# Reciprocal roots in the second layer of a graph network kernel: from an integer trick on VectorE to powers on GpSimd, with the planner's bookings re-set

## The chip, the cores and the metric

The kernel runs on one core of one Trainium2 chip. The metric is the device time in microseconds (us) of one execution. The core's engines run their own queues of instructions, each strictly in order: PE (TensorE, matmuls; PEld is its weight load), DVE (VectorE), ACT (ScalarE), POOL (GpSimd, which here also issues the indirect gathers) and SP (which issues plain DMAs). An instruction that waits for another engine holds up everything behind it in its own queue.

## The reference: what is computed

Two layers over a graph of 3125 nodes with 256 features and 50,000 edges (sorted by target). Layer 0 adds a graph convolution, a linear attention with an MLP, and a soft mixture of 8 experts. Layer 1, cut to what the change touches:

```python
xn = _layernorm(x)
x = x + gnn(xn, src, dst) + hyper(xn)        # edge attention with an MLP; hyperbolic branch
x = x + moe(_layernorm(x))                   # a shared MLP, and 2 of 8 private experts

# gnn: y = (softmax over a node's edges of clip(q.k), times v) @ Wp; x1 = feat + y
h = _layernorm(x1, ln_g, ln_b)               # reciprocal root of the variance: "g"
out = x1 + gelu(h @ W1.T + b1) @ W2.T + b2

# hyper: proj and logmap0 divide by the norm of a row, again and again
proj(x)    = where(n > maxnorm, x / n * maxnorm, x)
expmap0(u) = tanh(n) * u / n                 # n = norm of the row
logmap0(p) = arctanh(clip(n)) * p / n
```

In the kernel the hyperbolic branch needs three reciprocal norms per node, called nn, n3 and n4 after their tiles, each from a sum of squares that stands in a tile of 125 rows and 1 to 4 columns.

## The kernel before

The nodes are cut into 25 tiles of 125 rows, grouped into 7 chunks of four tiles (the last has one). x and its normed copy stay in SBUF.

*The planner.* The order of instructions isn't written out by hand. Each piece of work is a generator that yields `Op(engine, cost, after, take, give)` (line 68) ahead of the instructions that it issues. `Flow.run` (line 87 on) keeps, engine by engine, the time at which the engine would be free by these booked costs in us, adds 0.2 for each hand-over and 1.28 where ACT must load another function table, and always issues the op that could start first; ties go to the lower urgency. `take` and `give` name buffers with their counts. The booked costs thus decide only the order in which each engine's queue is filled; the chip then runs the queues in order at its own speed.

*Layer 0* (until some 1200 us). Per tile, 17 indirect gathers on POOL (L1063) fetch neighbour rows, and PE adds them up (L1092), in groups of six, six and five. Between them PE runs the layer's MLP (L683 and L697, stream `mlp_stream`, line 636) and then the soft experts (L1171 "fp0" and "fp1", L1183 "fy").

*Layer 1, edges* (some 1205 to 2025 us). For each of 75 groups of five or six blocks of edges: POOL gathers k and v into one of three kvg buffers (L1504), PE expands q (L1540), DVE multiplies it with k (L1544), sums (L1563) and clips (L1568), ACT takes the exponential (L1570), DVE scales v (L1573), and PE sums into the target nodes (L1581). After the third group of a tile the sums are divided, turned and multiplied by Wp. Three streams run beside it:

- `mlp_stream` with name "g": mean and variance per tile (L644, L645), the chunk's reciprocal root (L650, L651), the normed rows (L654), turning, the up-projection hp_g (L683) with a gelu on ACT (L675), the down-projection dn_g (L697). The same function serves layer 0 under the name "m".
- `hyper`, tile by tile, with the root nn for each pair of tiles (L1671 to L1674), a division of 512 columns on DVE (L1684), and transposes and matmuls on PE (cat, oT, ft).
- `hyper_end`, chunk by chunk, with the roots n3 (L1718 to L1720) and n4 (L1733 to L1739).

*Layer 1, experts*. When all chunks are normed again (`route_in`), the router sorts rows to experts, POOL scatters them, and PE runs 32 blocks of two private experts' matmuls (L2059, L2074). The shared MLP (`shared`, L1985 and L1999) fills PE meanwhile.

*The root*, `rsqrt` (line 287), is a bit trick and three Newton rounds, all on DVE: a shift and a multiply-add on integers (L291, L292) and three times L295, L296, L297. It is called with 1 to 4 columns; the caller books 2.1 or 2.3 us for it with its neighbours.

Of the kernel before, what the change touches and what calls it, by code (L numbers as in the profile page):

```python
# [7 lines left out]
F32 = mybir.dt.float32  # L8
# [3 lines left out]
OP = mybir.AluOpType  # L12
# [8 lines left out]
P = 125  # L21
# [129 lines left out]
def kernel(ctx: ExitStack, tc: tile.TileContext, a: dict, out: bass.AP):  # L151
# [71 lines left out]
    def row(pool, name, parts=P):  # L223
# [41 lines left out]
    part = keep.tile([128, 1], F32, name="part")  # L265
    nc.gpsimd.iota(part, pattern=[[0, 1]], base=0, channel_multiplier=1,
                   allow_small_or_imprecise_dtypes=True)
    tiny = keep.tile([128, 1], F32, name="tiny")
    nc.vector.memset(tiny, 1e-15)
    rank8 = keep.tile([P, NE], F32, name="rank8")  # L270
# [15 lines left out]

    def rsqrt(v, n, name, parts=P):

        y = small.tile([parts, n], F32, tag=f"rsy{n}", name=f"rsy_{name}", bufs=6)
        g = small.tile([parts, n], F32, tag=f"rsg{n}", name=f"rsg_{name}", bufs=6)  # L290
        nc.vector.tensor_scalar(g.bitcast(I32), v.bitcast(I32), 1, None, op0=OP.arith_shift_right)  # L291
        nc.vector.tensor_scalar(y.bitcast(I32), g.bitcast(I32), -1, 0x5F3759DF,  # L292
                                op0=OP.mult, op1=OP.add)
        for _ in range(3):
            nc.vector.scalar_tensor_tensor(g, y, -0.5, v, op0=OP.mult, op1=OP.mult)  # L295
            nc.vector.tensor_tensor(g, g, y, OP.mult)  # L296
            nc.vector.scalar_tensor_tensor(y, g, 1.5, y, op0=OP.add, op1=OP.mult)  # L297
        return y

    def turned(dst_, src_, nt, name, nk=2, g=None, b=None):  # L300

# [334 lines left out]
    def mlp_stream(c, inputs, name, pool_of, w1, w2, g, b, b1, done, start=None):  # L636

        t0, nt = CHUNKS[c]
        n = nt * P
        mv = small.tile([P, 4, 2], F32, tag=f"mv_{name}", name=f"mv_{name}{c}", bufs=2)  # L640
        for j in range(nt):
            m = yield Op("DVE", 0.6, [inputs[t0 + j]])
            st = small.tile([P, 6], F32, tag="st", name=f"st_{name}{c}_{j}")
            nc.vector.bn_stats(st, XN[c][:, j, :])  # L644
            nc.vector.bn_aggr(mv[:, j, :], st)  # L645
            m2 = yield Op("DVE", 0.42, [m])
            nc.vector.tensor_tensor(X[c][:, j, :], X[c][:, j, :], XN[c][:, j, :], OP.add)
        m = yield Op("DVE", 2.1, [m])
        var = small.tile([P, 4], F32, tag="rs", name=f"var_{name}{c}")
        nc.vector.tensor_scalar(var[:, :nt], mv[:, :nt, 1], 1e-5, None, op0=OP.add)  # L650
        rs = rsqrt(var[:, :nt], nt, f"{name}{c}")  # L651
        for j in range(nt):
            m = yield Op("DVE", 0.36, [m, m2])
            nc.vector.tensor_scalar(XN[c][:, j, :], XN[c][:, j, :], mv[:, j, 0:1],  # L654
                                    rs[:, j : j + 1], op0=OP.subtract, op1=OP.mult)
        both = []
        mk = yield Op("PE", 0.48 * nt, [m] + ([start] if start else []), take=["mm", "mm", "mlp"])
        pt = [mm_tile([128, 512], f"tr_{name}_{c}_{k}") for k in range(2)]
        for k in range(2):
            for j in range(nt):  # L660
                nc.tensor.transpose(pt[k][:, j * P : (j + 1) * P],
                                    XN[c][:, j, k * 128 : (k + 1) * 128], ident[:P, :P])
        for k in range(2):
            m = yield Op("ACT", 0.56, [mk], take=["hT"] if k == 0 else [], give=["mm"])
            if k == 0:
                hT = pool_of().tile([128, 2, 4 * P], F32, tag="hT", name=f"hT_{name}_{c}")
            nc.scalar.activation(hT[:, k, :n], pt[k][:, :n], AF.Identity,
                                 bias=col(b, k), scale=col(g, k))
        hid, todo, acts = [], [], []
        def gelu():  # L670
            mk, ps, q = todo.pop(0)
            act = yield Op("ACT", 0.75, [mk], give=["mm"], table="gelu")
            acts.append(act)
            hm = pool_of().tile([128, 4 * P], F32, tag="hid", name=f"hid_{name}{c}_{q}", bufs=8)
            nc.scalar.activation(hm[:, :n], ps[:, :n], AF.Gelu, bias=col(b1, q))  # L675
            hid.append(hm)

        for h in range(8):
            mk = yield Op("PE", 0.0035 * n, [m], take=["mm", "hid"],
                          give=["hT", "mlp"] if h == 7 else [])  # L680
            ps = mm_tile([128, 512], f"hp_{name}{c}_{h}")
            for k in range(2):
                nc.tensor.matmul(ps[:, :n], w1[:, k, h * 128 : (h + 1) * 128], hT[:, k, :n],  # L683
                                 start=(k == 0), stop=(k == 1))
# [758 lines left out]
    def layer1(lists):  # L1443
# [23 lines left out]
        for m in range(6):  # L1467
# [9 lines left out]

        flow = Flow(kvg=3, S=3, Sb=2, ST=2, q3=2, qe=2, ed=1, mm=2, nm=3, z=1, cat=2, r=2,
                    oT=1, ft=5, ch=2, sc=1, mlp=1, hT=1, hid=8,
                    mh=8, rhid=8, rw=2, xr=2, xrT=2, yr=2, to=3)  # L1480
        attended_ = [Mark() for _ in range(T)]
        mlp_, hyp_ = [Mark() for _ in CHUNKS], [Mark() for _ in CHUNKS]

# [128 lines left out]
        def hyper(t, pair, ch):  # L1612
# [6 lines left out]
            if t == t0:  # L1619
# [1 line left out]
                z = pair["z"] = lp.tile([128, 6, 2 * P], F32, tag="z", name=f"z_{t}")  # L1621
                nc.sync.dma_start(out=z[:, :, : nt * P], in_=ztab[:, :, t0 * P : (t0 + nt) * P])
                for i in range(6):
                    mk = yield Op("ACT", 0.43, [m])
                    nc.scalar.activation(z[:, i, : nt * P], z[:, i, : nt * P], AF.Relu,
                                         bias=bh[:, i : i + 1], scale=bs[:, i : i + 1])
                pair["ready"].set(mk)
# [4 lines left out]
            for i in range(4):  # L1632
                s, h = divmod(i, 2)
                last = i == 3 and t == t0 + nt - 1
                mk = yield Op("PE", 0.75 if s == 0 else 1.4, [pair["ready"]],
                              take=["nm"] + (["cat"] if i == 0 else []),
                              give=["z"] if last else [])
                po = nm_tile([P, 3, 128], f"cat_{t}_{i}")
# [27 lines left out]
                                    AX.X, OP.add)  # L1666
            s12 = ch["s12"][:, j : j + 1]
            if t == t0 + nt - 1:
                m = yield Op("DVE", 2.3, [m, full])
                nn = lp.tile([P, 2], F32, tag="nn", name=f"nn_{t}", bufs=2)[:, :nt]  # L1670
                nc.vector.tensor_reduce(nn, pair["n2"][:, :nt, :], AX.X, OP.add)  # L1671
                nc.vector.tensor_scalar(nn, nn, MIN_NORM ** 2, None, op0=OP.max)
                y = rsqrt(nn, nt, f"nn{t}")
                nc.vector.tensor_scalar(ch["s12"][:, j + 1 - nt : j + 1], y, ATANH_MAXN, 1.0,  # L1674
                                        op0=OP.mult, op1=OP.min)
                pair["scale"].set(m)
# [5 lines left out]
            for q in range(2):  # L1682
# [10 lines left out]
            sq = lp.tile([P, 512], BF16, tag="sq", name=f"sq3_{t}")  # L1693
            nc.scalar.activation(sq, r.rearrange("p q d -> p (q d)"), AF.Square,
                                 accum_out=ch["n3"][:, j : j + 1])
            m = yield Op("PE", 0.96, [m], take=["mm"], give=["r"])
            pt = mm_tile([128, 4, P], f"oT_{t}")
            for k in range(4):
                nc.tensor.transpose(pt[:, k, :], r[:, k, :], ident[:P, :P])
# [13 lines left out]

        def hyper_end(c, ch):
            t0, nt = CHUNKS[c]
            m = yield Op("DVE", 2.3, ch["done"])
            n3, s3, n4 = ch["n3"][:, :nt], ch["s3"][:, :nt], ch["n4"][:, :nt]
            nc.vector.tensor_scalar(n3, n3, MIN_NORM ** 2, None, op0=OP.max)  # L1718
            y = rsqrt(n3, nt, f"n3{c}")
            nc.vector.tensor_scalar(s3, y, ATANH_MAXN, 1.0, op0=OP.mult, op1=OP.min)  # L1720
            ends = []
            for j in range(nt):
# [4 lines left out]
            for j in range(nt):  # L1727
# [1 line left out]
                sq = lp.tile([P, 512], BF16, tag="sq", name=f"sq4_{t0 + j}")  # L1729
                nc.scalar.activation(sq[:, :C], ch["ft"][j], AF.Square,  # L1730
                                     accum_out=ch["n4"][:, j : j + 1])
            m = yield Op("DVE", 2.3, [m])
            nc.vector.tensor_scalar(n4, n4, MIN_NORM ** 2, None, op0=OP.max)  # L1733
            y = rsqrt(n4, nt, f"n4{c}")
            nc.vector.tensor_tensor(n4, n4, y, OP.mult)
            m = yield Op("ACT", 0.22, [m])
            nc.scalar.activation(n4, n4, AF.Tanh)
# [230 lines left out]
        def shared(c):  # L1968
# [10 lines left out]

            for h in range(8):  # L1980
                tag = ("mm", "qe")[h % 2]
                mk = yield Op("PE", 0.0035 * n, [turned_[c], moe_], take=[tag, "mh"])
                ps = ps_tile(tag, [128, 512], f"hp_s{c}_{h}")
                for k in range(2):
                    nc.tensor.matmul(ps[:, :n], R["w1"][:, k, h * 128 : (h + 1) * 128],  # L1985
# [4 lines left out]
            for j in range(nt):  # L1990
                for q in range(0, 8, 4):
                    if j == 0 and q == 4:
                        yield from gelu()
                    m = yield Op("PE", 1.75, [acts[q + 3]], take=["nm"] if q == 0 else [],
                                 give=["mh"] * 8 if j == nt - 1 and q == 4 else [])
                    if q == 0:
                        po = nm_tile([P, C], f"dn_s{c}_{j}")
                    for i in range(q, q + 4):
# [320 lines left out]
```

## Time and profile before

| | |
|---|---|
| median of 11 runs | 2757.36 us (2752.74 to 2761.26) |
| the profiled execution | 2755.13 us, its span 2753.3 us |
| busy over the span | PE 2496.5 us (91%), DVE 1389.6 (50%), POOL 1157.6 (42%), ACT 968.3 (35%) |
| mean granted PE clock | 0.966 |
| layer 0, gathers of POOL | 250.5 to 828 us |
| layer 1, first to last gather | 1229.2 to 1997.3 us |
| POOL gathers of layer 1, L1504 | 425, 461.1 us busy, 309.2 us of idle time before them |

How to read it: busy time is time in which an instruction ran. A row of a group gives the line, the engine, the operation, written and read tile, count, then busy us and mean ns, then the engine's idle time ahead of such instructions with what ended most of it. A row of waits gives who waited, `<-` for whom, us in total, how many times, and the longest. A wait for several events is put down to the last of them. PE's ends are modelled, so a busy PE isn't PE at its peak.

### The profile page before, as it was taken

To read this page: it belongs to the slowest core of one execution; us is meant where nothing else is said; L and a number is where in the kernel's file an instruction comes from. 1 tells how busy PE (TensorE), PEld (TensorE's weight loads), DVE (VectorE), ACT (ScalarE), POOL (GpSimd) and SP (SyncE) were. 2 spreads that over 40 slices of the span, in tenths; PEclk is the share of its full clock that TensorE was granted. 3 is DMA by queue.
4 is the path that set the end of the run, shared out by engine and by line. 5 is a ranking of instruction groups with operands and counts; after the bars stand their busy time and mean duration, and the time that the engine had idled before them with its cause. 6 is when DMAs were issued, how large, how long until landed. Compare 5 with 4: busy or idle time off the path is not lost. (4 is left out here: it accounts for less than half of the span.)

```text
span 2753.3 us, 32241 instructions
## 1 busy us (share of the span) xinstructions
PE 2496.5 (91%) x11409; PEld 1816.6 (66%) x11409; DVE 1389.6 (50%) x3497; ACT 968.3 (35%) x2001; POOL 1157.6 (42%) x1145
## 2 busy tenths in 40 slices
PE   4889989999999999987778888889898999999998
PEld 3556776666666555565556666667576678888885
DVE  6365123453633334267898888888886101111103
ACT  4773112232223333344335444444532222222221
POOL 3002777777770000025665655565601822222220
PEclk9989989999999999998899999999999999999999
DMA  4425565576661015137676655565610355555545
GB/s 111 154 91 175 169 211 165 166 218 177 206 183 35 1 56 149 37 97 249 203 225 193 209 186 181 185 213 176 211 46 1 85 186 188 197 198 188 195 144 144
DMA packets 186968, 427.01 MB, mean 155 GB/s; under 512 B 31403, under 2 KB 116523, under 8 KB 178604
## 3 DMA queue, kind: packets, MB, share of 16 engines
q0 software_dynamic: 80688, 281.78, 33.1%
q1 hardware_dynamic: 103448, 140.79, 16.2%
q10 hardware_dynamic: 2660, 2.29, 0.3%
q8 instruction: 92, 1.51, 0.2%
q14 instruction: 80, 0.66, 0.1%
HBM read 358.95 MB, written 65.74 MB: 154 GB/s over the span
## 5 line engine op out<-in xcount | busy, mean ns | idle before, releaser
L1504 POOL DMA_INDIRECT kvg<-kvtab,el x425 | 461.1, 1085 | 309.2 <-issue 103.7
L1063 POOL DMA_INDIRECT msg<-hs,el x425 | 421.7, 992 | 322.0 <-DMA hot<-S 190.6
L1175 ACT ACTIVATE fh<-fp,bnh,bns 128x500 f32<-128x500 f32 (+1 forms) x224 | 160.7, 723 | 372.6 <-PE fp L1171 370.8
L1581 PE MATMUL es<-kvg,S 128*125 128x264 f32 x850 | 220.2, 411 | 51.1 <-DVE kvg L1573 50.6
L2047 ACT ACTIVATE rhid<-rh,rw 128x256 f32<-128x256 f32 x256 | 121.5, 474 | 338.2 <-PE rh L2059 338.2
L2059 PE MATMUL rh<-xrT,rw 128*128 128x256 f32 x1024 | 237.4, 380 | 0.0
L2074 PE MATMUL ry<-rw,rhid 128*128 128x256 f32 x1024 | 231.5, 379 | 0.0
L1186 DVE SCALAR_TENSOR_TENSOR x<-fy,f_w,x 125x256 f32<-125x256 f32 x200 | 96.2, 482 | 262.2 <-PE fy L1183 261.7
L1581 PEld LDWEIGHTS es<-kvg,S 128*125 128x125 f32 x850 | 163.3, 198 | 98.1 <-DVE kvg L1573 67.0
L1092 PEld LDWEIGHTS <-S 128*125 128x125 bf16 x1275 | 153.3, 138 | 94.5 <-issue 82.5
L1540 PE MATMUL qe<-q,ST 125*128 125x256 bf16 x1275 | 173.1, 277 | 44.8 <-DVE kvg L1544 39.0
L2074 PEld LDWEIGHTS ry<-rw,rhid 128*128 128x128 f32 x1024 | 194.6, 190 | 26.9 <-issue 0.5
L2059 PEld LDWEIGHTS rh<-xrT,rw 128*128 128x128 f32 x1024 | 189.7, 190 | 28.6 <-ACT rhid L2047 5.0
L2081 DVE TENSOR_TENSOR yr<-ry,rw 128x256 f32<-128x256 f32 x64 | 27.2, 424 | 357.7 <-PE ry L2074 357.7
L1183 PE MATMUL fy<-f_Wo,fh 128*125 128x256 f32 x800 | 205.3, 380 | 1.2 <-DVE x L1186 0.8
L1092 PE MATMUL es<-msg,S 128*125 128x256 bf16 x1275 | 183.1, 276 | 24.7 <-DMA msg<-hs,el 23.9
L1171 PE MATMUL fp<-fh,f_W 128*128 128x500 f32 (+1 forms) x448 | 187.0, 545 | 0.3 <-ACT fh L1175 0.3
L1171 PE MATMUL fp<-xT_f,f_W 128*128 128x500 f32 (+1 forms) x448 | 186.0, 541 | 0.0
L1540 PEld LDWEIGHTS <-ST 125*128 125x128 bf16 x1275 | 125.5, 99 | 81.4 <-issue 48.6
L1183 PEld LDWEIGHTS fy<-f_Wo,fh 128*125 128x125 f32 x800 | 142.2, 188 | 55.9 <-issue 34.4
L1299 POOL TENSOR_TENSOR xn<-xn,row_bp 125x1024 f32<-125x1024 f32 (+1 forms) x7 | 13.8, 1977 | 379.8 <-DVE hx L1273 192.5
L1544 DVE TENSOR_TENSOR kvg<-qe,kvg 128x512 f32<-128x512 f32 (+1 forms) x225 | 142.8, 651 | 26.5 <-PE qe L1540 21.1
(422 smaller groups left out, 4225.4 us busy)
## 6 DMA issues: line engine op xcount, KB each, us to landing
db<-dlT SPq DMA_DIRECT2D x25, 544.0 KB
ST<-dlT SPq DMA_DIRECT2D x25, 544.0 KB
hot<-S SPq DMA_DIRECT2D x50, 187.5 KB
Sb<-hot SPq DMA_DIRECT2D x50, 187.5 KB
ztab<-z SPq DMA_DIRECT2D x18, 500.0 KB
z<-ztab SPq DMA_DIRECT2D x12, 750.0 KB
xs<-pad SPq DMA_DIRECT2D x1, 8224.0 KB
xr<-xs SPq DMA_DIRECT2D x32, 257.0 KB
```

Source lines behind the costliest of these rows:

```text
L1063: nc.gpsimd.indirect_dma_start(out=msg[:, i, :], out_offset=None, in_=hs3_rows, in_offset=bass.IndirectOffsetOnAxis(ap=el[:, b, g0 + i : g ...
L1092: nc.tensor.matmul(blk["po"], S[:, i, :], msg[:, i, r * C : (r + 1) * C], start=(g0 + i == 0 and r == 0), stop=(g0 + i == LE - 1 and r == 2))
L1171: nc.tensor.matmul(ps[q][:, :n], self.ws[e][i][:, k, q * 128 : (q + 1) * 128], h[:, k, :n], start=(k == 0), stop=(k == 1))
L1175: nc.scalar.activation(nxt[:, q, :n], ps[q][:, :n], AF.Relu, bias=self.sh[i][:, 2 * e + q : 2 * e + q + 1], scale=self.sc[i][:, 2 * e + q ...
L1183: nc.tensor.matmul(po, nxt[:, k, j * P : (j + 1) * P], self.ws[e][2][:, k, :], start=(k == 0), stop=(k == 1))
L1504: nc.gpsimd.indirect_dma_start(out=kvg[:, i, : 2 * C], out_offset=None, in_=kvtab, in_offset=bass.IndirectOffsetOnAxis(ap=el[:, b, g0 + i ...
L1540: nc.tensor.matmul(pq[i0][:, i, :], ST[:P, g0 + i0 + i, :], blk["q3"][:, r, :], start=(r == 0), stop=(r == 2))
L1544: nc.vector.tensor_tensor(kvg[:, i0 : i0 + k, :C], pq[i0][:, :k, :], kvg[:, i0 : i0 + k, :C], OP.mult)
L1581: nc.tensor.matmul(blk["pa"], S[:, i, :], kvg[:, i, C:], start=(g0 + i == 0), stop=(g0 + i == LE - 1))
L2047: nc.scalar.activation(hid[-1][:, q % 2, :], ps, AF.Gelu, bias=w1[:, 8 * C + q : 8 * C + q + 1])
L2059: nc.tensor.matmul(ps, w1[:, k * 4 * C + h * 128 : k * 4 * C + (h + 1) * 128], xrT[:, k, :], start=(k == 0), stop=(k == 1))
L2074: nc.tensor.matmul(po, hid[k // 2][:, k % 2, r * 128 : (r + 1) * 128], w2[:, k * C : (k + 1) * C], start=(k == 0), stop=(k == 7))
```

## The change

It has two halves. In layer 1 the four kinds of root (nn, n3, n4, and the variance of the MLP "g") are taken by a new generator, `rsqrt_by_power`: POOL raises the operand to the power -0.5, elementwise, and DVE refines it by one Newton round of three instructions. As DVE and POOL now hand over, the one booked op of 2.1 or 2.3 us becomes up to four: the instructions ahead on DVE, the power on POOL (booked 0.65), the round on DVE (0.5), the instructions behind. Layer 0's MLP keeps `rsqrt`. Second, several bookings get other values: the up-projection of `mlp_stream` (both layers), the relu of the hyperbolic input, its transposes and matmuls; and the shared MLP takes a token "shared", so that only one chunk of it can be under way. Some small tiles get more buffers. The core of the diff:

```diff
+    minus_half = keep.tile([128, 4], F32, name="minus_half")
+    nc.vector.memset(minus_half, -0.5)
...
+    def rsqrt_by_power(v, n, name, m):
+
+        y = small.tile([P, n], F32, tag=f"rpy{n}", name=f"rpy_{name}", bufs=8)
+        g = small.tile([P, n], F32, tag=f"rpg{n}", name=f"rpg_{name}", bufs=8)
+        m = yield Op("POOL", 0.65, [m])
+        nc.gpsimd.tensor_tensor(y, v, minus_half[:P, :n], OP.pow)
+        m = yield Op("DVE", 0.5, [m])
+        nc.vector.scalar_tensor_tensor(g, y, -0.5, v, op0=OP.mult, op1=OP.mult)
+        nc.vector.tensor_tensor(g, g, y, OP.mult)
+        nc.vector.scalar_tensor_tensor(y, g, 1.5, y, op0=OP.add, op1=OP.mult)
+        return y, m
...
-        mv = small.tile([P, 4, 2], F32, tag=f"mv_{name}", name=f"mv_{name}{c}", bufs=2)
+        mv = small.tile([P, 4, 2], F32, tag="mmv", name=f"mv_{name}{c}", bufs=len(CHUNKS))
...
+        if name == "m":
+            m = yield Op("DVE", 2.1, [m])
...
+        else:
+            m = yield Op("DVE", 0.17, [m])
+            var = small.tile([P, 4], F32, tag="mvar", name=f"var_{name}{c}", bufs=len(CHUNKS))
+            nc.vector.tensor_scalar(var[:, :nt], mv[:, :nt, 1], 1e-5, None, op0=OP.add)
+            rs, m = yield from rsqrt_by_power(var[:, :nt], nt, f"{name}{c}", m)
...
-            mk = yield Op("PE", 0.0035 * n, [m], take=["mm", "hid"],
+            mk = yield Op("PE", 0.0039 * n, [m], take=["mm", "hid"],
...
-                    mh=8, rhid=8, rw=2, xr=2, xrT=2, yr=2, to=3)
+                    mh=8, shared=1, rhid=8, rw=2, xr=2, xrT=2, yr=2, to=3)
...
-                    mk = yield Op("ACT", 0.43, [m])
+                    mk = yield Op("ACT", 0.55, [m])
...
-                mk = yield Op("PE", 0.75 if s == 0 else 1.4, [pair["ready"]],
+                mk = yield Op("PE", 0.48 if s == 0 else 0.86, [pair["ready"]],
...
-                m = yield Op("DVE", 2.3, [m, full])
+                m = yield Op("DVE", 0.4, [m, full])
...
-                y = rsqrt(nn, nt, f"nn{t}")
+                y, m = yield from rsqrt_by_power(nn, nt, f"nn{t}", m)
+                m = yield Op("DVE", 0.17, [m])
...
-            m = yield Op("PE", 0.96, [m], take=["mm"], give=["r"])
+            m = yield Op("PE", 0.62, [m], take=["mm"], give=["r"])
...
-            m = yield Op("DVE", 2.3, ch["done"])
+            m = yield Op("DVE", 0.17, ch["done"])
...
-            y = rsqrt(n3, nt, f"n3{c}")
+            y, m = yield from rsqrt_by_power(n3, nt, f"n3{c}", m)
+            m = yield Op("DVE", 0.17, [m])
...
-            m = yield Op("DVE", 2.3, [m])
+            m = yield Op("DVE", 0.17, [m])
...
-            y = rsqrt(n4, nt, f"n4{c}")
+            y, m = yield from rsqrt_by_power(n4, nt, f"n4{c}", m)
+            m = yield Op("DVE", 0.17, [m])
...
-                mk = yield Op("PE", 0.0035 * n, [turned_[c], moe_], take=[tag, "mh"])
+                mk = yield Op("PE", 0.0035 * n, [turned_[c], moe_],
+                              take=[tag, "mh"] + (["shared"] if h == 0 else []))
...
-                                 give=["mh"] * 8 if j == nt - 1 and q == 4 else [])
+                                 give=["mh"] * 8 + ["shared"] if j == nt - 1 and q == 4 else [])
```

More of the change, by code (lines that the diff above doesn't have):

```diff
@@ L287, in rsqrt @@
     def rsqrt(v, n, name, parts=P):
-        y = small.tile([parts, n], F32, tag=f"rsy{n}", name=f"rsy_{name}", bufs=6)
-        g = small.tile([parts, n], F32, tag=f"rsg{n}", name=f"rsg_{name}", bufs=6)
+        y = small.tile([parts, n], F32, tag=f"rsy{n}", name=f"rsy_{name}", bufs=6 if n < 9 else 1)
+        g = small.tile([parts, n], F32, tag=f"rsg{n}", name=f"rsg_{name}", bufs=6 if n < 9 else 1)
         nc.vector.tensor_scalar(g.bitcast(I32), v.bitcast(I32), 1, None, op0=OP.arith_shift_right)
@@ L647, in mlp_stream @@
             nc.vector.tensor_tensor(X[c][:, j, :], X[c][:, j, :], XN[c][:, j, :], OP.add)
[L648 to L651, printed above, removed]
+        if name == "m":
+            m = yield Op("DVE", 2.1, [m])
+            var = small.tile([P, 4], F32, tag="rs", name=f"var_{name}{c}")
+            nc.vector.tensor_scalar(var[:, :nt], mv[:, :nt, 1], 1e-5, None, op0=OP.add)
+            rs = rsqrt(var[:, :nt], nt, f"{name}{c}")
+        else:
+            m = yield Op("DVE", 0.17, [m])
+            var = small.tile([P, 4], F32, tag="mvar", name=f"var_{name}{c}", bufs=len(CHUNKS))
+            nc.vector.tensor_scalar(var[:, :nt], mv[:, :nt, 1], 1e-5, None, op0=OP.add)
+            rs, m = yield from rsqrt_by_power(var[:, :nt], nt, f"{name}{c}", m)
         for j in range(nt):
```

## The prediction

> **What bounds the kernel now.** I read the table of windows first, because shares of the whole span mix two layers and the experts. Columns: window, its length, then busy us (and instructions) of PE, PEld, DVE, ACT and POOL, then PE's granted clock, DMA share, GB/s.
>
> ```profile
> 1300.00:1400.00 100.00, 72.02 (x391) 55.75 (x389) 80.92 (x157) 36.84 (x103) 63.83 (x58) 0.88 0.69 213
> 1400.00:1500.00 100.00, 82.69 (x441) 61.46 (x442) 92.76 (x166) 48.76 (x112) 62.53 (x58) 0.93 0.65 204
> ...
> 2200.00:2400.00 200.00, 194.79 (x900) 166.16 (x899) 21.51 (x53) 48.05 (x100) 55.65 (x60) 0.98 0.54 190
> 2400.00:2600.00 200.00, 200.00 (x954) 174.61 (x953) 22.61 (x56) 53.15 (x112) 55.35 (x56) 1.00 0.55 194
> ```
>
> Behind 2130 us PE is the bound (busy 605.6 of 624 us), and between 400 and 1200 us too (96% to 100%). From 1300 to 2000 us, the second layer's edges, it isn't: seven such windows sum to DVE 614.5 busy of 700, PE 585.2, so PE idles 114.8 us. PE's work behind that stage is fixed, so what shortens the stage should reach the end. Whom PE waits for is in its list of waits, 1300 to 2000 us (total, times, longest):
>
> ```profile
> PE es L1581 <- DVE kvg L1573: 40.6, 43, 3.4
> PE qe L1540 <- DVE kvg L1544: 36.3, 38, 5.3
> PE hp_g L683 <- ACT hT_g L667: 14.3, 3, 5.0
> ```
>
> The first two rows, with three small ones, make 81 of the 115 us. So DVE is the engine to relieve. Its own 85 us of idle are waits for ACT above all:
>
> ```profile
> DVE r L1684 <- ACT r L1681: 22.8, 10, 3.9
> DVE sums L1592 <- ACT sums L1589: 10.3, 11, 2.1
> ```
>
> **The roots on DVE.** The old root is 11 dependent small instructions. Three of their groups in the same stretch (busy, mean ns, then idle before them):
>
> ```profile
> L295 DVE SCALAR_TENSOR_TENSOR rsg_nn<-rsy_nn,nn 125x2 f32<-125x2 f32 x33 | 5.4, 162 | 1.1
> ...
> L295 DVE SCALAR_TENSOR_TENSOR rsg_g<-rsy_g,var_g 125x4 f32<-125x4 f32 x15 | 2.5, 163 | 0.5
> ...
> L291 DVE TENSOR_SCALAR rsg_nn<-nn 125x2 int32<-125x2 int32 x11 | 1.9, 169 | 0.4
> ```
>
> One takes 162 ns and 33 ns pass before it (1.1 us over 33): a step of 0.195 us, as the timeline has it (2076.53, 2076.72, 2076.92). The new root keeps three on DVE; eight go: 8 x 0.195 = 1.56 us. There are 34 roots: 13 of nn, and 7 each of n3, n4 and the MLP's variance. The counts put 11 nn (x11), 5 variances (x15 over three rounds) and 10 n3 and n4 into 1300 to 2000: 26 x 1.56 = **40.6 us** off DVE there. The other eight stand ahead of 1300 or behind 2000. I count them at nothing: behind 2000 PE has its MLP work (118.8 of 130 us busy to 2130); without that cover they would be 8 x 1.56 = 12 us more gain.
>
> How much of 40.6 arrives: at least the share of PE's idle that DVE causes, 81/115 or 28 us, at most all. What is late next is ACT (32 us of PE's idle) and PE itself, 585 us of work in some 665. I take **-35**.
>
> **The power on POOL.** The trace has no power. Bounds: below, POOL's 1x1 memset, 0.09 us; above, its 125x1024 addition, 2.36 us. Nearest is the other two-input form, the 125x256 addition at 0.73 us: I take that. POOL then leaves 0.30 us to the next instruction (the gathers' "issue", 103.7 us over 340). So 1.03 us per root, 27 us in the stage. POOL's gathers there idle 309 us, of which 205 are waits for a free buffer: these cover it. Without that cover, about one gather group in three would start 1 us later.
>
> The Trainium skill, "GPSIMD Engine Reference", 2.1 Instruction dispatch, speaks against this change: the first call into a freshly loaded POOL kernel costs some 6 us without an instruction in the profile. If gathers and powers displaced each other, 34 x 6 would be 204 us of POOL and, by an estimate from that page, a slower kernel. The rows speak against it for additions: between two gathers the 125x1024 addition (L1070) takes 2.36 us, and behind another addition (L1302) 2.39. No row shows it for a power.
>
> **The new wait.** DVE's Newton round now waits for POOL. In the built order of the changed kernel, 0 to 58 other DVE instructions stand between the operand and its round. Summed by the durations of their rows, 24 roots have 3 us or more of such cover. Ten have less: nn1 1.7, nn11 0.2, g2 0.8, g3 1.9, g4 2.4, nn19 0.8, n34 0, nn23 1.7, n35 2.1, n45 0.8, sum 12.4. With POOL free, 1.03 us exposes five of them, 2.6 us in all. If each power stood behind a whole group of six gathers, 6 x (1.085 + 0.30) = 8.3 us, it would be 10 x 9.3 - 12.4 = 81 us. Queued behind the waiting round on DVE are the products (L1544, L1573) that PE waits for, so a stall there is one of the stage. The planner books a group at 8.1 us, near 8.3, and queues a power behind groups that it holds for done, so I stay near the lower end: **+5**, and keep both ends.
>
> **Table loads on ACT.** The new order scatters the MLP's gelus among the edges' exponentials: in the built order the table loads between the first and the last edge group rise from 28 to 41. At 1.283 us each (today's ACT_TABLE_LOAD rows) that is 16.7 us more of ACT, busy 45% there. Bounds 0 and 16.7. Today's 28 loads, 36 us, stand beside 13 us of waits for exponentials or gelus (DVE 4.5 on L1570, PE 8.6 on hid_g), not all from loads: I take a quarter, **+4**.
>
> **Layer 0 moves too.** The booking of the up-projection (0.0035 n to 0.0039 n) is shared by both layers' MLPs, so layer 0's order changes: ahead of its last edge sum PE now has 2 fp0, 4 fp1, 4 fy and 8 transposes less. By rows: 6 x 0.83 (187.0 us over 448 records, two each) + 4 x 0.51 + 0.9 = 8 us of PE work more behind that sum (0.9 for eight transposes by the timeline). When the sum comes is POOL's to say:
>
> ```profile
> L1063 POOL DMA_INDIRECT msg<-hs,el x425 | 421.7, 992 | 322.0 <-DMA hot<-S 190.6 <-issue 113.9 <-PE es L1092 9.7
> ```
>
> Without the first wait, 421.7 + 131.4 us of gathers and 24 us of additions fill all of 250 to 828 us: POOL can't be earlier, and PE, with less to do in between, waits (today 23.9 us, 29 times, for msg). PE can win back what it is behind the data today, some 2 us at most: a group of gathers lasts 7.5, of which the landing (3.2) and the sums (2.5) leave 1.8, and POOL hardly waits for PE. Bounds 6 and 8; **+7**.
>
> **The order itself.** Lower bookings of the hyperbolic transposes fit their rows better (three take 3 x 0.174 = 0.52 us busy, booked 0.75, now 0.48). What other placements give can't be read off a row. I take **0**, between -15 and +15: three waits for hT_g alone were worth 14.3 us. The guard "shared" leaves the sequence of the shared MLP's chunks as it was, and more buffers for mv and var only loosen waits of DVE on itself.
>
> **Sum.** -35 + 5 + 4 + 7 + 0 = -19 us. The profiled execution took 2755.1 us (span 2753.3): 2736. The median of the runs shown, 2757.4, lies 2.3 higher, so I predict **2738 us**. Its own range: good ends (-41, +2, 0, +6, -10) and poor ones (-28, +8, +8, +8) make -43 and -4, so 2714 to 2753.
>
> **Rivals.**
> - *The gain is eaten*: DVE's relief gives only 28, all 13 loads show (+16.7), layer 0 costs 8, POOL 5: +2, **2759 us**. For it: ACT causes 40 of DVE's 85 us of idle. Against: ACT is idle over half of the stage.
> - *DVE waits behind gathers, slower*: the ten short roots find POOL on average half a group late, 4.2 + 1.03 - 1.24 = 4 us each, 40 us instead of 5: -35 + 40 + 4 + 7 = +16, **2773 us**; at a whole group (81) +57. It cancels the gain from 2.4 us per short root and makes a slower kernel from 3.0. For it: POOL is an in-order queue and waits 205 us for buffers, so a power can stand behind a gather that isn't allowed to start. Against: the planner's bookings are close to the rows.
> - *It doesn't do what it says* can't be: 272 fewer DVE instructions stand in the built order. Only the power's price is open, and it acts through the second rival.
>
> **How the numbers follow.** Forecast 0.62, eaten 0.18, slower 0.20. This kernel's measurement can tell about 0.2%, 5.5 us, from no change. Faster: 0.60 + 0.02 of the second; same: 0.02 + 0.15; slower: 0.20 + 0.01. The range goes from 2705 (the good ends, with all of the order's 15 and 4 of the 12 us outside the stage) to 2773, the middle of the third case; that leaves about 2 in 10 out.
>
> **What would show it.** Right: in the second layer's edges DVE's busy time falls by some 35 us and the stage by 20 to 30; the L1573 and L1544 waits of PE shrink; powers take 0.3 to 1 us; 41 table loads; the last edge sum of layer 0 still near 833 us and the start of the second layer's gathers (1229) some 7 us later. Wrong: DVE waits for POOL of more than 25 us in sum, powers of several us, or a stage as long as before.

## The result and the profile after

The changed kernel is **slower**: 2766.79 us (median of 14 runs) against 2756.04 us for the kernel before beside it (53 runs), ratio 1.0037 [1.0026, 1.0047]. A second set of runs gave 1.0038 [1.0022, 1.0054]. I had forecast 2738 us. In three of the five groups of experiments below the kernel before itself took 2906 to 2925 us, at a mean granted PE clock of 0.93 to 0.95 instead of some 0.96; ratios there are read within their group alone.

In the changed kernel's listing, lines of the edge loop stand 20 lines further down (L1573 is L1593), those of the hyperbolic branch 21 (L1684 is L1705), later ones up to 24.

The page of the changed kernel, its span, the engines' totals, and POOL's gathers of both layers:

```profile
span 2764.9 us, 32042 instructions
...
PE 2497.6 (90%) x11409; PEld 1819.8 (66%) x11409; DVE 1343.2 (49%) x3226; ACT 982.8 (36%) x2013; POOL 1194.5 (43%) x1179
...
L1524 POOL DMA_INDIRECT kvg<-kvtab,el x425 | 467.3, 1100 | 226.0 <-issue 112.6
L1083 POOL DMA_INDIRECT msg<-hs,el x425 | 419.9, 988 | 324.1 <-DMA hot<-S 195.7
```

DVE has 46.4 us less to do (1389.6 before), as meant. The span is 11.6 us longer all the same. Where the edges run shows it best. I take the stage from the first gather of the second layer to its last edge sum; first before, then after (columns as in the prediction: window, length, then busy us of PE, PEld, DVE, ACT, POOL):

```profile
1229.00:2026.00 797.00, 655.74 (x3505) 504.93 (x3505) 687.37 (x1316) 353.93 (x875) 461.12 (x425) 0.94 0.63 198
```

```profile
1236.00:2041.00 805.00, 663.52 (x3519) 513.82 (x3518) 645.43 (x1070) 369.20 (x889) 496.49 (x454) 0.92 0.63 196
```

The stage begins 7 us later, and with 42 us less on DVE it lasts 8 us longer; from the last edge sum to the end it then takes 724 us for 727.5. What DVE does with the freed time stands in its waits of the changed kernel, 1300 to 2000 us (total, times, longest):

```profile
DVE kvg L1593 <- ACT kvg L1590: 27.2, 21, 6.1
DVE sums L1612 <- ACT sums L1609: 18.1, 14, 3.2
...
DVE rpg_n L309 <- POOL rpy_n L307: 11.9, 7, 4.3
DVE rpg_nn L309 <- POOL rpy_nn L307: 9.8, 5, 2.7
...
DVE rpg_g L309 <- POOL rpy_g L307: 8.1, 3, 4.1
...
DVE r L1705 <- ACT r L1702: 1.1, 3, 0.4
```

Waits for r have gone (22.8 before), but waits for the exponential came in their place (L1570 before: 4.5 us, now 27.2), and there are three rows that did not exist, the waits for the power. PE, which should have been served sooner, waits longer for scaled values than before (40.6 us) and a little less for products (36.3):

```profile
PE es L1601 <- DVE kvg L1593: 46.1, 39, 6.8
PE qe L1560 <- DVE kvg L1564: 28.4, 25, 2.8
PE oT L1720 <- DVE r L1712: 15.0, 3, 8.4
```

### The profile page after: what moved, and what is told of

It reads as the page before. It is cut to its first block, busy times and chain, and to the rows that moved or that the text cites. A ratio compares the mean times of both kernels' runs of the same rounds, so it can differ in the third digit from the quotient of the medians.

```text
span 2764.9 us, 32042 instructions
## 1 busy us (share of the span) xinstructions
PE 2497.6 (90%) x11409; PEld 1819.8 (66%) x11409; DVE 1343.2 (49%) x3226; ACT 982.8 (36%) x2013; POOL 1194.5 (43%) x1179
## 5 line engine op out<-in xcount | busy, mean ns | idle before, releaser
L1524 POOL DMA_INDIRECT kvg<-kvtab,el x425 | 467.3, 1100 | 226.0 <-issue 112.6
L2105 DVE TENSOR_TENSOR yr<-ry,rw 128x256 f32<-128x256 f32 x64 | 27.2, 424 | 357.4 <-PE ry L2098 357.4
```

The lines of the kernel that those rows point to most:

```text
L1524: nc.gpsimd.indirect_dma_start(out=kvg[:, i, : 2 * C], out_offset=None, in_=kvtab, in_offset=bass.IndirectOffsetOnAxis(ap=el[:, b, g0 + i ...
```

## The experiments

**Theories.** (1) DVE's relief is real, but handing the root to POOL and back eats it. (2) The stage isn't bound by DVE at all; the loop gather, scores, product, exponential, scaling, sum over three kvg buffers holds it, whatever DVE does. (3) The bookings, and so the re-laid order, do the harm. The kernels came in five groups, each on one chip beside runs of the kernel before.

| group, kernel before (us) | kernel | us | ratio to before |
|---|---|---|---|
| A, 2910.26 | k_oneround | 2903.72 | 0.9990 [0.9962, 1.0018] |
| | f_seed | 2918.29 | 1.0047 [1.0015, 1.0080] |
| | b_powers | 2930.63 | 1.0072 [1.0042, 1.0103] |
| | a_bookings | 2914.51 | 1.0016 [0.9986, 1.0045] |
| B, 2905.63 | k_oneround2 | 2894.30 | 0.9965 [0.9937, 0.9993] |
| | n_fiveround | 2937.26 | 1.0109 [1.0077, 1.0142] |
| | m_table | 2935.02 | 1.0103 [1.0067, 1.0139] |
| | g_lag | 2920.83 | 1.0041 [1.0020, 1.0061] |
| C, 2753.61 | after_again | 2764.51 | 1.0038 [1.0022, 1.0054] |
| | f_seed2 | 2749.87 | 0.9984 [0.9973, 0.9995] |
| | k_oneround3 | 2741.44 | 0.9950 [0.9932, 0.9969] |
| | r_inplace | 2805.68 | 1.0187 [1.0168, 1.0207] |
| D, 2925.04 | s_layer0 | 2941.07 | 1.0056 [1.0034, 1.0077] |
| | v_seed | 2938.20 | 1.0056 [1.0035, 1.0077] |
| | g_lag2 | 2940.95 | 1.0035 [1.0008, 1.0062] |
| | n_fiveround2 | 2949.36 | 1.0079 [1.0055, 1.0104] |
| E, 2756.74 | c_layer0 | 2754.03 | 0.9994 [0.9979, 1.0010] |
| | g_lag3 | 2736.10 | 0.9929 [0.9905, 0.9953] |

**DVE's time alone, both ways.** In the kernel before, order and bookings untouched, the four kinds of root get one Newton round (or five) in place of three.

```diff
-    def rsqrt(v, n, name, parts=P):
+    def rsqrt(v, n, name, parts=P, rounds=3):
...
-        for _ in range(3):
+        for _ in range(rounds):
...
-                y = rsqrt(nn, nt, f"nn{t}")
+                y = rsqrt(nn, nt, f"nn{t}", rounds=1)
```

> The kernel before, its order and bookings unchanged, but every root of the second layer's g norms, nn, n3 and n4 with one Newton round in place of three (6 VectorE instructions fewer per root, nothing on GpSimd). VectorE's busy time falls by about 31 us (1389.6 to 1358.8 in an earlier run of the same kernel, where a whole-kernel ratio of 0.9990 [0.9962, 1.0018] left it open what that is worth). Theory 1 (VectorE's instructions bound the second layer's edge stretch, first to last es of the second layer 763.2 us before): that stretch becomes 20 to 30 us shorter and the whole ratio is 0.989 to 0.993. Theory 2 (the stretch is held by the loop gather, scores, product, exponential, scaling, edge sum over three kvg buffers; VectorE's work stands in its gaps): the stretch moves by under 6 us, ratio 0.998 to 1.001.

> The mirror of the one-round kernel: the kernel before, order and bookings unchanged, with five Newton rounds in place of three in the same roots (6 VectorE instructions more per root, VectorE some 31 us busier). Theory 1: the edge stretch 20 to 30 us longer, ratio 1.007 to 1.011. Theory 2: within 6 us, ratio 0.999 to 1.002.

In one group, 34.5 us less on DVE (1389.6 to 1355.1) brought 11.3 us; 29.9 us more cost 31.6:

```profile
PE 2543.8 (87%) x11409; PEld 1837.5 (63%) x11409; DVE 1419.5 (49%) x3701; ACT 967.4 (33%) x2001; POOL 1146.9 (39%) x1145
```

So theory 2 is out: DVE's work stands on the path, since added work counts about in full (five rounds ran only in groups B and D). It does so behind the stage too: from the last edge sum to the end the five-round kernels take 735 and 736 us, the one-round kernel 725. Removed work, though, counts for a third. The first and third run of the one-round kernel gave 6.5 and 12.2 us (0.9990, 0.9950), a fifth and 37% of what DVE lost; none of the three runs reached the 22 us that I had put down for a stage bound by DVE. Its stage in group C is 10 us shorter, and says why:

```profile
1229.00:2016.00 787.00, 656.40 (x3506) 508.07 (x3506) 660.74 (x1138) 353.34 (x876) 465.21 (x425) 0.93 0.64 200
```

DVE is busy 26.6 us less, but its waits grow. Its waits in that stage:

```profile
DVE r L1684 <- ACT r L1681: 28.7, 10, 5.4
...
DVE kvg L1573 <- ACT kvg L1570: 15.0, 19, 2.6
DVE sums L1592 <- ACT sums L1589: 14.4, 15, 2.1
```

Before they are 22.8, 5.5 and 10.3 us in the same stage. All waits of DVE for ACT grow from 42.1 to 62.6 us: DVE arrives earlier and stands at ACT. ACT is busy for 353 of the 787 us, so it isn't full; why its results come late there isn't followed further.

**The square: order against seed.** Group C sets two orders (before's, the changed one) against two ways to get the seed (POOL's power; DVE's two integer instructions), with one Newton round in all four. f_seed2 is the changed kernel with

```diff
-        nc.gpsimd.tensor_tensor(y, v, minus_half[:P, :n], OP.pow)
+        nc.vector.tensor_scalar(g.bitcast(I32), v.bitcast(I32), 1, None, op0=OP.arith_shift_right)
+        nc.vector.tensor_scalar(y.bitcast(I32), g.bitcast(I32), -1, 0x5F3759DF,
+                                op0=OP.mult, op1=OP.add)
```

and r_inplace is the kernel before, no booking altered, with a call that issues power and round at once:

```diff
-                y = rsqrt(nn, nt, f"nn{t}")
+                y = rsqrt_by_power(nn, nt, f"nn{t}")
```

> The changed kernel itself, unaltered, on the same chip as the other three of this group, so that each can be set against it. The four make a square: order of before or re-laid order, root's seed by power on GpSimd or by two VectorE instructions, one Newton round in all. Measured against before it should stand near its first ratio, 1.0037 [1.0026, 1.0047]. Theory 1 (handing the root to GpSimd and back eats the relief): this kernel 0.4 to 1% slower than the same order with the seed on VectorE. Theory 3 (the re-laid order does the harm): within 0.2% of it.

> The changed kernel's order on all engines, but where the power stood VectorE computes the seed with its two integer instructions; GpSimd has no power and nobody waits for one. One Newton round as in the change. (An earlier run of the same kernel: 1.0047 [1.0015, 1.0080] against before.) Theory 1: 0.4 to 1% faster than the changed kernel. Theory 3: as slow as the changed kernel, 1.003 to 1.006 against before, and 0.4 to 0.8% slower than the one-round kernel in the order of before.

> The order of before with one Newton round in the second layer's roots, seed on VectorE. (Earlier runs of the same kernel: 0.9990 [0.9962, 1.0018] and 0.9965 [0.9937, 0.9993].) Both theories: 0.995 to 0.999 against before, the fastest of the four.

> The order of before with no booking altered, where each root of the second layer's g norms, nn, n3 and n4 is at its place the power on GpSimd and the one Newton round on VectorE, with no other VectorE work planned between them: VectorE stands at each until the power is back. Theory 1: 41 round trips of 1 to 3 us, of which a part falls on waits that are there anyway: 0.4 to 1.2% slower than the one-round kernel, 1.001 to 1.009 against before. Theory 3: within 0.3% of the one-round kernel, faster than or equal to before.

| us against before | seed on DVE | power on POOL |
|---|---|---|
| order of before | -12.2 | +52.1 |
| re-laid order | -3.7 | +10.9 |

In the re-laid order the power costs 14.6 us more than two DVE instructions would; in the old order, where nothing is planned between power and round, 64 us. That is far more than I had expected of r_inplace (1.001 to 1.009, where I wrote 41 round trips; there are 34 roots). The new order by itself costs 8.4 us (seed on DVE). So theories 1 and 3 each hold a part here, theory 1 the larger: -12.2 + 8.4 + 14.6 = +10.8, which is the changed kernel's 10.9 by construction and no check of it. In group A the same two kernels with the seed on DVE lie 14.6 us apart (2918.29 and 2903.72): the size of the order's price is that of group C alone. r_inplace shows the price of the hand-over plainly in its waits, 1219 to 2079 us:

```profile
DVE rpg_n L307 <- POOL rpy_n L306: 52.2, 12, 9.7
DVE rpg_nn L307 <- POOL rpy_nn L306: 45.6, 12, 7.8
...
DVE rpg_g L307 <- POOL rpy_g L306: 14.6, 6, 7.6
```

112 us of standing in 30 waits, up to 9.7 us each. Where POOL was free, DVE waits 0.8 to 1.2 us; in every wait over 1.3 us the power starts within 0.03 us of the end of a gather, so it stood behind gathers. One such wait in the changed kernel, in the timelines of POOL and of DVE (start, us; idle before in brackets):

```profile
1624.62 1.61 POOL L1524 DMA_INDIRECT kvg<-kvtab,el  x1 [0.30 <-issue]
1626.53 1.16 POOL L1524 DMA_INDIRECT kvg<-kvtab,el  x1 [0.30 <-issue]
1628.00 0.95 POOL L1524 DMA_INDIRECT kvg<-kvtab,el  x1 [0.31 <-PE es L1601]
1629.25 0.94 POOL L1524 DMA_INDIRECT kvg<-kvtab,el  x1 [0.30 <-issue]
1630.22 1.05 POOL L307 TENSOR_TENSOR rpy_n<-n,minus_half 125x4 f32<-125x4 f32 x1
```

```profile
1623.26 0.16 DVE L1739 TENSOR_SCALAR n<-n 125x4 f32<-125x4 f32 x1
...
1626.79 0.16 DVE L670 TENSOR_SCALAR var_g<-mv_g 125x4 f32<-125x4 f32 x1
1631.30 0.16 DVE L309 SCALAR_TENSOR_TENSOR rpg_n<-rpy_n,n 125x4 f32<-125x4 f32 x1 [4.35 <-POOL rpy_n L307]
```

The operand is there at 1623.42, and DVE stands at its round from 1626.95. POOL has just begun the third-last gather of a group, and the power has no idle time before it: it stood in the queue. DVE loses 4.35 us for a power of 1.05.

The other direction is in the 14.6 us too. Before 7 of the 26 powers up to the last gather, POOL itself stands waiting for the operand, 57 us in all, with gathers behind it. Mostly those couldn't have started anyway. By the trace, a group of gathers with no power ahead of it starts 0.3 us after its buffer is free and the gather before it is done; the 20 groups behind powers start 0.3 to 3.6 us after, 12 us more in sum. How the 14.6 us divide between the two directions isn't measured.

**Where the order's 8 us sit.** a_bookings is the kernel before with the changed bookings and the shared token alone; b_powers the changed kernel with the old bookings of hp, relu z, cat and oT; c_layer0 the changed kernel, s_layer0 the f_seed kernel, with

```diff
-            mk = yield Op("PE", 0.0039 * n, [m], take=["mm", "hid"],
+            mk = yield Op("PE", (0.0035 if name == "m" else 0.0039) * n, [m], take=["mm", "hid"],
```

v_seed has the old bookings, and the whole root on DVE with one round, booked 0.7.

> The kernel before with only the new bookings and the token of the shared MLP, all roots on DVE as before; 44 table loads. If the bookings do the harm: layer 0 +7, start-up up to +8, loads: 2763 to 2775. If the powers do it: layer 0's +7 alone, 2761 to 2765, or less where the better-fitting bookings help.

> The changed kernel with the old bookings of the up-projection, the relu, the hyperbolic transposes and matmuls (0.0035 n, 0.43, 0.75 and 1.4, 0.96), so powers alone; 33 table loads between the first and last edge group instead of 41. If the bookings did the harm (layer 0 +7, start-up +8, table loads), 2735 to 2750. If the powers did it, 2757 to 2765: only layer 0's 7 us come back.

> The changed kernel with the first layer's MLP matmuls booked at their former 0.0035 us per row; the power and its bookings as in the change, no lag. If the first layer's order is worth its 7 us: 0.25% faster than the changed kernel, near 1.001 against before on a chip where the changed kernel has 1.0038. VectorE's waits for the power stay near 34 us.

> The re-laid order with the seed on VectorE (2749.87 us, 0.9984 against before in the square), and the first layer's MLP matmuls booked at their former 0.0035 us per row, so that the first layer's order is that of before. If the order's cost is the first layer's: 6 to 8 us faster than that kernel, about 2743 us where before is 2754, ratio 0.995 to 0.997. If the 8 us came from the second layer: no change, 0.998 to 0.999.

> One Newton round and the seed on VectorE, with the order laid out anew for the shorter root alone (0.7 us booked in place of 2.3); the bookings of the MLP matmuls, the hyperbolic relu, cat and oT are those of before. If the lower bookings of cat and oT cause the second layer's late start (first gather to first edge sum 33 us before, 40 to 42 with the changed bookings): that stretch is 33 us again, the first layer is as before, and the kernel is the fastest of all, 2732 to 2742 us where before is 2754, ratio 0.992 to 0.996. If re-laying an order is a lottery whatever is booked: anywhere from 0.995 to 1.003.

In f_seed2's profile the second layer's gathers begin 8.2 us later than in the one-round kernel of the old order (1237.5 and 1229.3), the stage is equally long (786.9 us in both), and the rest takes 3 us more. So in these two profiles the order's price is mostly the first layer's; within the stage a late start and a quicker run cancel.

*First layer.* c_layer0 comes to 0.9994 where the changed kernel has 1.0038: 12 us back, with intervals that leave some 5 either way. In the profiled executions its second layer's first gather starts at 1225.7 us, the changed kernel's at 1236.1 and 1239.3, before's at 1229.2. *Start of the second layer.* From its first gather to its first edge sum: 33.4 us before, and 32.7 to 34.4 in all other profiles with the old bookings of relu, cat and oT (one round, five rounds, r_inplace, b_powers, v_seed). With the changed bookings: 41.6 and 40.4 (the change), and 38.6 to 42.8 in the nine others, the one without any power (a_bookings, 39.3) among them. That is 5 to 9 us, and the second layer's bookings (hp among them, which goes with the others in b_powers and v_seed) are the cause. What they do is on ACT. From the timelines of DVE and ACT, the changed kernel, then before:

```profile
1264.87 0.19 DVE L1588 TENSOR_SCALAR sco<-sco 128x48 f32<-128x48 f32 x1
...
1271.34 3.03 ACT L1645 ACTIVATE z<-z,bh,bs 128x250 f32<-128x250 f32 x6 [3.25 <-DMA z<-ztab]
1274.38 1.28 ACT L1590 ACT_TABLE_LOAD   x1
1275.67 0.38 ACT L1590 ACTIVATE kvg<-sco 128x48 f32<-128x48 f32 x2
```

```profile
1257.22 0.19 DVE L1568 TENSOR_SCALAR sco<-sco 128x48 f32<-128x48 f32 x1
...
1259.27 1.28 ACT L1570 ACT_TABLE_LOAD   x1
1260.56 0.24 ACT L1570 ACTIVATE kvg<-sco 128x48 f32<-128x48 f32 x1
1262.82 3.03 ACT L1625 ACTIVATE z<-z,bh,bs 128x250 f32<-128x250 f32 x6 [2.01 <-DMA z<-ztab]
```

The second pair's six relus now stand ahead of the first exponential, and wait for their own load. The first clipped scores are there 29 us after the first gather in the changed kernel and 28 before, but their exponential starts 10.6 us later in place of 3.2. Beyond the start, from first to last edge sum, f_seed2 takes 746.3 us and the one-round kernel in the old order 752.1; in group A's profiles the same two take 818.3 and 818.9, so that the new order is the better one there isn't shown.

In groups A and D b_powers, s_layer0 and v_seed all came out 0.6 to 0.7% slower than before, against what I expected of them, while in group A the bookings alone can't be told from before (a_bookings, 1.0016 [0.9986, 1.0045]). v_seed is the oddest: one round, no power, the old bookings of hp, relu, cat and oT, and yet slower than before, where one round in the old order never was. Without the changed kernel beside them they can't be split further.

**Table loads.** m_table is the changed kernel with the planner's price of a table switch in the second layer raised (`flow.TABLE = 2.5`).

> The changed kernel, with one constant more: in the second layer's plan a switch of the activation table is booked at 2.5 us in place of 1.28, so that the planner keeps exponentials and the others more together. The order it lays out has 24 table loads between the first and the last exponential group in place of 40 (before: 28). Theory 1 (a part of the lost gain, some 15 to 25 us, is exponentials that stand behind table loads): 8 to 20 us faster than the changed kernel, and VectorE's wait for the exponential falls from 27 us to under 12. Theory 2 (the loop holds the stretch whatever stands in it): within 5 us of the changed kernel.

Its edge stage has 26 table loads, against 42 in the changed kernel's and 30 before. DVE's waits for the exponential are 11.2 us, as hoped, and those for the power only 5.7; yet it is 1.0103 against before, and slower than g_lag beside it. The changed kernel didn't run in that group, so whether m_table is faster than it isn't known. Nor do the loads explain all of DVE's waits for ACT: 62.6 us with 30 loads (one round, old order), 55.0 with 42 (f_seed2); its waits for the exponential alone are 15.0 and 29.8. That loads were what cost the time is not shown by any run.

**Planning the round later.** g_lag is c_layer0 with one number more:

```diff
-        m = yield Op("POOL", 0.65, [m])
+        m = yield Op("POOL", 0.65, [m], lag=4.0)
```

> The changed kernel with two bookings altered: the first layer's MLP matmuls at their former 0.0035 us per row (its order back to that of before), and the power on GpSimd with a lag of 4 us, so that the planner puts the Newton instructions later on VectorE, after other work. The order has 26 table loads among the exponentials in place of 40. Theory 1 (the gain was eaten by VectorE waiting for the power, 30 us, by exponentials, 23, and by the first layer's 7 us): VectorE's waits for the power fall under 12 us, and the kernel is 15 to 30 us faster than the changed one and 5 to 20 us faster than before. Theory 2 (the loop holds the stretch): only the first layer's 7 us come back, ratio to before 1.000 to 1.002.

> The changed kernel with the first layer's former booking and the power booked with a lag of 4 us, so that VectorE's Newton instructions are planned behind other work (an earlier run of the same kernel: 1.0041 [1.0020, 1.0061]). If the hand-over's 15 us are VectorE standing at the power: its waits for the power fall from 34 to under 12 us, and the kernel is 15 to 22 us faster than the changed one, 0.996 to 0.999 against before. If later Newton instructions only hand the delay on to those who wait for the scale: within 4 us of the changed kernel less the first layer's 7, 1.000 to 1.004.

> The same kernel with a lag of 4 us booked behind the power, and no other difference. If VectorE standing at the power is the hand-over's price: 10 to 16 us (0.35 to 0.6%) faster than the kernel without the lag. If the delay is only handed on to what waits for the scale, or the new order loses as much elsewhere: within 0.2% of it.

Side by side in group E: 2754.03 without the lag, **2736.10** with it, 18 us (ratios 0.9994 and 0.9929). The stage without and with it:

```profile
1226.00:2037.00 811.00, 665.49 (x3516) 516.30 (x3515) 644.90 (x1068) 367.92 (x886) 503.00 (x454) 0.92 0.63 194
```

```profile
1229.00:2002.00 773.00, 649.66 (x3516) 505.54 (x3516) 642.60 (x1065) 350.07 (x867) 489.57 (x454) 0.94 0.66 204
```

(The stage is 38 us shorter, but it begins 3 us later, and from the last edge sum to the end it takes 735 us for 726: 25 us between the two profiled executions, 2765.0 and 2739.5 us. These lie 11 and 3 us above their medians.) DVE's waits for the power fall from 33.3 us to one row:

```profile
DVE rpg_g L309 <- POOL rpy_g L307: 2.5, 2, 2.1
```

The lag moves more than the round: this order has 28 table loads for 42, and waits for the exponential fall from 29.8 to 18.4 us. How the 18 us divide is open. And g_lag beats both kernels only where before takes 2757 us: in groups B and D, with waits for the power of 1.1 us, it was 0.4% slower than before. The one-round kernel in the old order had no ratio above 1 in three groups. Why a laid-out order that wins at one level loses at the other stays open.

The first runs of two kernels, told above:

> The kernel before with its own order and bookings, but the 34 roots of the second layer take one Newton round instead of three on DVE (two rounds, 6 DVE instructions per root, are left out, so its roots are less exact). No GpSimd, no re-ordering. Theory 1 (the second layer's edges are DVE-bound, and the changed kernel gives the relief away again in new waits): 6 x 0.195 x 34 = 40 us less DVE, 31 us of it from 1300 to 2000; at 70% or more 22 to 31 us faster than before, about 2730 us. Theory 2 (the stage is held by the loop over the three kvg buffers and its hand-overs, DVE's busy share only looks like a bound): within 6 us of before.

> The changed kernel with its order and bookings as they are, but at the place of each power DVE does the two integer instructions of the old seed (GpSimd does nothing; the roots are those of one Newton round, two rounds are left out). Against the changed kernel this takes the hand-over to GpSimd away (30 us of DVE waits for powers and 60 us in which GpSimd waits with gathers behind it) and adds 2 x 0.195 x 34 = 13 us of DVE. Theory 1 with the hand-over as the eater: 2767 - 30 x 0.8 + 9, about 2750 or less. Theory 1 with the re-laid order as the eater (waits for exponentials and sums on ACT, late start-up, layer 0): 2765 to 2770, no gain. Theory 2: 2760 to 2770 as well, but then the one-round kernel of the old order is no faster than before.

n_fiveround2 repeated the five rounds: 1.0079, 24 us for 30.1 us of DVE.

> Order and bookings of before, five Newton rounds in the second layer's roots in place of three: VectorE some 30 us busier (an earlier run of the same kernel: 1.0109 [1.0077, 1.0142]). One round less time on VectorE gave 12 of 33 us. If the stretch is bound by VectorE's own work: 25 to 35 us slower, 1.009 to 1.013. If the value of VectorE's time is the same 40% both ways: 10 to 14 us slower, 1.004 to 1.005.

## Why the prediction was wrong

**What bounds the stage**, DVE, was right in one direction: five rounds instead of three cost about their full length, 32 and 24 us for 30. In the other it was not, and the forecast needed the other.

**"How much of 40.6 arrives: at least the share of PE's idle that DVE causes, 81/115 or 28 us ... I take -35"** is the step that failed first. The count was right (DVE 42 us less in the stage). But 33 us less of DVE in the old order gave 12 us, 37%. My lower bound took PE's waits for DVE as what DVE owes, without asking what DVE had waited for itself. I named ACT as next in line, and gave it no price: DVE's waits for it grew by 20 us. At 37%, an estimate, the changed kernel's 46 us would be worth 17. The eight roots outside the stage, put at nothing, are a small part of it: the changed kernel takes 3 us less behind the last edge sum.

**"The new wait ... I stay near the lower end: +5"** failed second. I measured DVE's cover against a free POOL and counted ten short roots; the profile has 16 waits and 32.2 us in the stage, mean 2.0 us. The square prices the power at +14.6, which also holds gathers held up behind powers, a term that I had taken as covered, and is net of the two DVE instructions that a power saves. The second rival had the mechanism (40 us of waits, powers behind gathers), and its +16 lies nearest to the outcome; it got there with a relief of 35 that didn't come and a wait that costs less than half of its length in the end. Its reason against, that "the planner's bookings are close to the rows", was too weak: in the wait shown above a gather takes 1.61 us instead of 0.95, the operand comes when most of a group is still to be issued, and DVE arrives early. Whether that is so in the other waits wasn't followed one by one.

**The power itself** was priced well: 0.73 us taken, and 0.73 measured for two columns, 1.04 for four, within the bounds but for two of 2.42 and 2.45 us against 2.36. The changed kernel's powers (count, then ns min/median/max, first and last start):

```profile
L307 POOL TENSOR_TENSOR rpy_n<-n,minus_half x14: 551/1042/2417, 1384.2 to 2087.7; 125x4 f32<-125x4 f32 x12, 125x1 f32<-125x1 f32 x2
L307 POOL TENSOR_TENSOR rpy_nn<-nn,minus_half x13: 555/732/795, 1269.6 to 2053.3; 125x2 f32<-125x2 f32 x12, 125x1 f32<-125x1 f32 x1
L307 POOL TENSOR_TENSOR rpy_g<-var_g,minus_half x7: 551/1034/2448, 1418.5 to 2048.6; 125x4 f32<-125x4 f32 x6, 125x1 f32<-125x1 f32 x1
```

The power at 1630.22 starts 0.03 us after the gather ahead of it ends, and the gather behind the next power starts 0.18 us after that one. All 34 powers start within 0.2 us of the later of two times, that of their operand and the end of the instruction before them on POOL. The first-call price of some 6 us in the Trainium skill's "GPSIMD Engine Reference", 2.1 Instruction dispatch, does not show ahead of any of them.

**Layer 0, +7**, was right: first gather of the second layer at 1236.1 for 1229.2, last edge sum of layer 0 at 833.3 for 832.5; undoing that booking gave 12 us, give or take 5.

**Table loads, +4**: the count was nearly right (12 more in the stage for 13), a cost isn't shown.

**The order itself, 0**: the late start, 5 to 9 us, was in the built order to be read (relus ahead of the first exponential on ACT) and I had not looked there. In group C's profiles the order gains some 6 us back behind it. That the second layer's order came out near 0 in f_seed2 is luck: two parts cancel, and I had seen neither.

**The signs named**: DVE's busy time, the powers and the late start of layer 1 came as forecast; the shorter stage didn't, and two of the three signs of "wrong" appeared (waits for POOL over 25 us, a stage as long as before).

## What to carry to other kernels

Where an in-order schedule has been laid out for given durations, work taken off the busiest engine can give back a fraction of its length (here 21 to 37%), while work added to it costs most or all of it (here 81 and 106%); price both directions apart, and ask what that engine will wait for next. Before a short step moves to an engine that runs long batches, ask where in the batch it will stand, not how long it takes. Planning its consumer that much later took the waits away here, and was faster in the one group where both kernels ran. And look at the start of each stage in the built order: a booking changed for the middle can put other work ahead of the stage's first hand-over.

## What was not expected of the hardware

A power on POOL grew with its columns, at 125 rows: 0.55 us for one, 0.73 for two, 1.04 for four, some 0.16 us per column. And the same program stood at two levels: 2754 to 2757 us in two groups, 2906 to 2925 in three, once on one and the same chip; in the profiles of the one-round kernel the granted clock at the upper level is lower (0.944 for 0.965) and both edge stages are longer (layer 0's gathers 650 us from first to last for 574, layer 1's stage 846 for 787), while from the last edge sum of layer 1 to the end it takes 725 us at either level. What sets the level isn't known.
